# Four 3x3 convolutions: from direct taps over whole images to row-pair combinations over strips of 16 rows

## The chip, the cores and the metric

The kernel runs on one core of a Trainium2 chip. Time is device microseconds of that core, from three runs of the kernel before and one profiled execution. A core has a matrix engine (TensorE, PE in the profile; its weight loads are PEld), a vector engine (VectorE, DVE), a scalar engine (ScalarE, ACT), a general engine (GpSimd, POOL), and a queue engine (SyncE, SP), which here issues all transfers. TensorE reads SBUF and writes PSUM, which has eight banks of 512 float32 words on each of 128 partitions.

## The reference

The input `x` is 4 images of 64 channels and 128x128 pixels in float32. Four layers follow each other, and only the third and the head of the fourth are touched:

```
layer 0   a state-space layer over the pixels        x  -> x1
layer 1   windowed transforms and small matrices     x1 -> x2
layer 2   r = relu(bn(conv3x3(x2)));  r = relu(bn(conv3x3(r)))
          sums over the squares r[j:, j:], j = 0..64; their means, a 3-wide
          filter over channels, a sigmoid, a mean over j:  gate per image and channel
          x3 = relu(r * gate + x2)
layer 3   y = relu(conv3x3(x3));  t = conv3x3(y)      (64 -> 64 channels, padding 1)
          a state-space layer over t, then a feed-forward layer, then + x3
```

So four 3x3 convolutions of 64 to 64 channels are computed on four images. The gate needs the whole result of the second before the third can begin.

## The kernel before

The layers run one after another, with memory (DRAM) between them. `layer2_convs3` holds layer 2 and the two convolutions of layer 3. Images go in pairs: 2 images x 64 channels lie on the 128 partitions. Two buffers of a whole padded image pair (130 x 130 words on each partition) stand in SBUF, and the convolutions go from one to the other and back (`a` and `bb`).

`_conv` (line 1184) takes 8 rows at a time. For each of the nine taps it issues four matmuls of 64x64 weights by 512 pixels: two images (the two row halves of the array) by two groups of four rows (the two column halves). Nine taps add up in PSUM. The function `done` takes the result out: for the first three convolutions ACT writes relu(scale * p + bias) into the other image buffer (line 1258), for the fourth DVE adds the bias (line 1316), and 16 rows at a time are stored.

Between the second and the third convolution of a pair stands the gate. DVE takes the sums over the square rings, one row part (line 1283) and one column part (line 1284) for each of 64 rings, and one block (line 1280). A cumulative sum, a matmul with a band matrix and a sigmoid give a number for each partition. Then 8 rows at a time are fetched from memory again (line 1303), multiplied and added (line 1304), rectified in place (line 1305) and stored as `x3` (line 1306). The third convolution starts as soon as its first rows are there.

The program is recorded as a flow of tiles. A planner then sets the order of instructions on each engine, by data, by the buffers that are free and by its own estimate of when something is ready. An engine runs its instructions in that order and waits at each until its data are there. All transfers are issued by SP in one order, so a transfer that waits holds back those behind it.

Of the kernel before, what the change touches and what calls it, by code (L numbers as in the profile page):

```python
# [10 lines left out]
F32 = mybir.dt.float32  # L11
AF = mybir.ActivationFunctionType
ALU = mybir.AluOpType
AX = mybir.AxisListType
PSUM = bass.MemoryType.PSUM
DRAM = bass.MemoryType.DRAM

P = 128
B, C, HH, WW = 4, 64, 128, 128
# [97 lines left out]
class _Consts:  # L117


    def __init__(self, nc, pool, cst, upto=None):  # L120
        w = _OFF[upto][1] if upto else _CONST.shape[1]
        self.t = pool.tile([P, w], F32, name="cst")
        nc.sync.dma_start(self.t, cst[:, :w])
# [14 lines left out]
def _rstd(nc, out, in_, eps):  # L138

    nc.scalar.activation(out, in_, AF.Ln, bias=eps)  # L140
    nc.scalar.activation(out, out, AF.Exp, scale=-0.5)
# [29 lines left out]
class _Mamba:  # L171
# [119 lines left out]
    def rows(self, bc, h, k):  # L291

        a = 64 * h + DD * k if self.small else 64 * (h ^ k)
        return bc[a : a + self.nst, :512] if self.small else bc[a : a + self.nst, _COLS[h]]
# [365 lines left out]
    def gated(self, c):  # L660

        yg = self.tmp("yg")
        self.nc.vector.tensor_mul(yg, c["y"], c["sz"])
        return yg
# [514 lines left out]


RW = WW + 2


def _conv(tc, pool, W, src, done):

    nc = tc.nc
    half = [slice(64 * h, 64 * (h + 1)) for h in range(2)]
    for r in range(0, HH, 8):  # L1190
        p = [pool.tile([P, 4, WW], F32, name=f"cv{i}", tag=f"cv{i}") for i in range(2)]
        for k in range(9):
            dy, dx = divmod(k, 3)
            for h in range(2):
                at = r + 4 * h + dy
                for i in range(2):
                    nc.tensor.matmul(  # L1197
                        p[i][half[h]],
                        W[half[i], k, :],
                        src[half[i], at : at + 4, dx : dx + WW],  # L1200
                        start=k == 0,
                        stop=k == 8,
                    )
        for i in range(2):
            for h in range(2):
                done(i, r + 4 * h, h, p[i][half[h]])


@with_exitstack
def layer2_convs3(ctx, tc, K, w, w3, x2, x3, t3):  # L1210
    nc = tc.nc
    cp = ctx.enter_context(tc.tile_pool(name="l2c", bufs=1))
    wp = ctx.enter_context(tc.tile_pool(name="l2w", bufs=3))
    cv = ctx.enter_context(tc.tile_pool(name="l2p", bufs=3, space=PSUM))
    sm = ctx.enter_context(tc.tile_pool(name="l2s", bufs=1, space=PSUM))

    wts = []
    for src in (w["c1"], w["c2"], w3["c1"], w3["c2"]):
        t = cp.tile([P, 9, C], F32, name=f"cw{len(wts)}")
        for h in range(2):  # L1220
            nc.sync.dma_start(t[64 * h : 64 * (h + 1)], src)
        wts.append(t)
    eps = cp.tile([P, 1], F32, name="eps2")
    nc.vector.memset(eps, 1e-5)
    norms = []
    for i in "12":
        g, b, m, v, cb = (
            _dup(nc, cp, w[k], f"{k}_") for k in (f"bn{i}_g", f"bn{i}_b", f"bn{i}_m", f"bn{i}_v", f"c{i}_b")
        )
        _rstd(nc, v, v, eps)  # L1230
        nc.vector.tensor_mul(g, g, v)
        nc.vector.tensor_sub(cb, cb, m)
        nc.vector.tensor_mul(cb, cb, g)
        nc.vector.tensor_add(cb, cb, b)
        norms.append((g, cb))
    bias3 = [_dup(nc, cp, w3[k], f"{k}3") for k in ("c1_b", "c2_b")]
    eca = cp.tile([P, 3], F32, name="eca")
    nc.sync.dma_start(eca, w["eca"].to_broadcast([P, 3]))
    band = cp.tile([P, P], F32, name="band")
    nc.vector.tensor_scalar(band, K.sh0, eca[:, 0:1], None, ALU.mult)  # L1240
    nc.vector.scalar_tensor_tensor(band, K.sh1, eca[:, 1:2], band, ALU.mult, ALU.add)
    nc.vector.scalar_tensor_tensor(band, K.sh2, eca[:, 2:3], band, ALU.mult, ALU.add)

    bufs = []
    for i in range(2):
        t = cp.tile([P, HH + 2, RW], F32, name=f"img{i}")
        nc.gpsimd.memset(t[:, 0:1, :], 0.0)
        nc.gpsimd.memset(t[:, HH + 1 : HH + 2, :], 0.0)
        nc.gpsimd.memset(t[:, :, 0:1], 0.0)
        nc.gpsimd.memset(t[:, :, RW - 1 : RW], 0.0)  # L1250
        bufs.append(t)
    a, bb = bufs
    ain, bin_ = (t[:, 1 : HH + 1, 1 : WW + 1] for t in bufs)

    def into(dst, func, scale, bias):
        def done(i, r, h, p):
            at = slice(64 * h, 64 * (h + 1))
            nc.scalar.activation(
                dst[64 * i : 64 * (i + 1), r : r + 4, :],
                p,  # L1260
                func,
                scale=scale if isinstance(scale, float) else scale[at],
                bias=bias[at],
            )

        return done

    NSUM = HH // 2 + 1
    for pr in range(B // 2):
        img2 = x2[2 * pr : 2 * pr + 2].rearrange("b c (r w) -> (b c) r w", w=WW)  # L1270
        img3 = x3[2 * pr : 2 * pr + 2].rearrange("b c (r w) -> (b c) r w", w=WW)
        for r in range(0, HH, 32):
            nc.sync.dma_start(ain[:, r : r + 32, :], img2[:, r : r + 32, :])
        _conv(tc, cv, wts[0], a, into(bin_, AF.Relu, *norms[0]))
        _conv(tc, cv, wts[1], bb, into(ain, AF.Relu, *norms[1]))


        part = wp.tile([P, 2, NSUM], F32, name="part", tag="part")
        nc.vector.memset(part[:, 1, 0:1], 0.0)
        nc.vector.tensor_reduce(part[:, 0, 0:1], ain[:, HH // 2 :, WW // 2 :], AX.XY, ALU.add)  # L1280
        for i in range(1, NSUM):
            j = HH // 2 - i
            nc.vector.tensor_reduce(part[:, 0, i : i + 1], ain[:, j, j:], AX.X, ALU.add)
            nc.vector.tensor_reduce(part[:, 1, i : i + 1], ain[:, j + 1 :, j], AX.X, ALU.add)
        add = wp.tile([P, NSUM], F32, name="add", tag="add")
        nc.vector.tensor_add(add, part[:, 0, :], part[:, 1, :])
        sq = wp.tile([P, NSUM], F32, name="sq", tag="sq")
        nc.vector.tensor_tensor_scan(sq, K.ones[:, :NSUM], add, 0.0, ALU.mult, ALU.add)

        nc.vector.tensor_mul(sq, sq, K.iarea)  # L1290
        py = sm.tile([P, NSUM], F32, name="py", tag="py")
        nc.tensor.matmul(py, band, sq, start=True, stop=True)
        sg = wp.tile([P, NSUM], F32, name="sg", tag="sg")
        nc.scalar.activation(sg, py, AF.Sigmoid)
        nc.vector.tensor_mul(sg, sg, sq)
        gate = wp.tile([P, 1], F32, name="gate", tag="gate")
        nc.vector.tensor_reduce(gate, sg, AX.X, ALU.add)
        nc.vector.tensor_scalar_mul(gate, gate, 1.0 / NSUM)

        for r in range(0, HH, 8):  # L1300
            rows = slice(r, r + 8)
            res = wp.tile([P, 8, WW], F32, name="res2", tag="res2")
            nc.sync.dma_start(res, img2[:, rows, :])
            nc.vector.scalar_tensor_tensor(res, ain[:, rows, :], gate, res, ALU.mult, ALU.add)
            nc.scalar.activation(ain[:, rows, :], res, AF.Relu)
            nc.sync.dma_start(img3[:, rows, :], ain[:, rows, :])

        _conv(tc, cv, wts[2], a, into(bin_, AF.Relu, 1.0, bias3[0]))
        tok = t3[2 * pr : 2 * pr + 2].rearrange("b c (r w) -> (b c) r w", w=WW)
        stage = {}  # L1310

        def store(i, r, h, p):
            at = slice(64 * h, 64 * (h + 1))
            if r % 16 == 0 and i == 0:
                stage["t"] = wp.tile([P, 16, WW], F32, name="tok", tag="tok", bufs=2)
            nc.vector.tensor_scalar(
                stage["t"][64 * i : 64 * (i + 1), r % 16 : r % 16 + 4, :], p, bias3[1][at], None, ALU.add
            )
            if r % 16 == 12 and i == 1:
                nc.sync.dma_start(tok[:, r - 12 : r + 4, :], stage["t"])  # L1320

        _conv(tc, cv, wts[3], bb, store)

# [105 lines left out]
def layer3_ffn(ctx, tc, K, w, n3, s3, out):  # L1431
# [46 lines left out]
    def first(b, r0, H):  # L1478
# [15 lines left out]
        for t in (1, 0):  # L1494
            himg = H[t] = wp.tile([P, R + 2, RW], F32, name=f"h{t}", tag=f"h{t}")
            nc.gpsimd.memset(himg[:, :, 0:1], 0.0)  # L1496
            nc.gpsimd.memset(himg[:, :, RW - 1 : RW], 0.0)
            if r0 == 0:
# [210 lines left out]
```

## Time and profile before

| | us |
|---|---|
| median of 3 runs | 17,647.88 (17,646.33 to 17,652.58) |
| profiled execution, its time | 17,656.56 |
| its span, first to last instruction | 17,654.7 |
| convolution stage, first to last matmul of line 1197 | 4332.8 to 5418.7 |
| PE busy in the span | 14,230.1 |
| DVE busy | 15,333.9 |
| ACT busy | 14,311.2 |
| POOL busy | 13,820.2 |

How to read a row of the groups of instructions: line of the kernel, engine, operation, tile written <- tiles read (partitions x elements), count; then busy time in us and the mean of one in ns; then the time that its engine sat idle just before, and what ended most of that. Up to about 3,160 us the span belongs to layer 0, from 5,422 us on to the rest of layer 3, both with DVE, ACT and POOL busy most of the time.

### The profile page before, as it was taken

The numbers are of one execution on the slowest core, as the hardware profiler recorded it, in microseconds if no ns is written. First come the engines' busy times: TensorE is split into PE (matmuls) and PEld (weight loads), VectorE is DVE, ScalarE is ACT, GpSimd is POOL, SyncE is SP. The second block draws the span as 40 slices with busy tenths as digits, with TensorE's granted clock in tenths as the row PEclk, the third lists the DMA queues.
The fourth block names the chain that finished last, engine by engine and source line by source line (L and its number), as shares of the span: only waits on it lengthen the run. The fifth ranks groups of instructions, "written<-read, shape, count | busy, mean of one in ns | idle before, by whom it ended". The sixth has DMA issues, their size and how long they took to land. (4 is left out here: it accounts for less than half of the span.)

```text
span 17654.7 us, 242673 instructions
## 1 busy us (share of the span) xinstructions
PE 14230.1 (81%) x82490; PEld 6984.1 (40%) x82490; DVE 15333.9 (87%) x8623; ACT 14311.2 (81%) x29985; POOL 13820.2 (78%) x7966
## 2 busy tenths in 40 slices
PE   7888888798997777777777777777777777777799
PEld 3333333387334333333333333333333333333333
DVE  8999999522216999999999999999999999999977
ACT  8999999112335999999999999999999999999733
POOL 7999999200005999999999999999999999999700
PEclk8888888799998999999999999999999999999899
DMA  6766666111212333333333333333333333333222
GB/s 160 179 179 178 175 179 177 51 61 45 72 41 79 89 90 91 88 93 85 93 85 94 83 95 84 94 86 91 87 91 86 93 87 91 89 90 91 69 59 55
DMA packets 669699, 1723.23 MB, mean 98 GB/s; under 512 B 196816, under 2 KB 232096, under 8 KB 661024
## 3 DMA queue, kind: packets, MB, share of 16 engines
q1 hardware_dynamic: 668448, 1707.69, 36.0%
q8 instruction: 646, 10.58, 0.3%
q14 instruction: 605, 4.96, 0.1%
HBM read 1434.33 MB, written 272.63 MB: 97 GB/s over the span
## 5 line engine op out<-in xcount | busy, mean ns | idle before, releaser
L632 POOL TENSOR_TENSOR ring<-ring,cb 128x1024 f32<-128x1024 f32 x5120 | 12038.9, 2381 | 335.4 <-DVE ring L626 186.1
L626 DVE TENSOR_TENSOR_SCAN ring<-da,state,bx 128x1024 f32<-128x1024 f32 x4848 | 11053.0, 2327 | 70.8 <-PE y L457 38.1
L431 ACT ACTIVATE bxT<-duT,BT 128x128 f32<-128x128 f32 x21504 | 6706.0, 389 | 29.9 <-PE bx L514 28.1
L582 ACT ACTIVATE da<-dl,A 128x1024 f32<-128x1024 f32 x5120 | 5751.0, 1139 | 168.1 <-DVE ring L626 115.2
L514 PE MATMUL bx<-cst,bxT 128*128 128x128 f32 x24576 | 3693.7, 300 | 945.1 <-DVE ring L626 641.6
L514 PEld LDWEIGHTS bx<-cst,bxT 128*128 128x128 f32 x24576 | 3248.7, 209 | 2341.9 <-DVE ring L626 1523.1
L520 PE MATMUL bx<-bc,spread 64*128 64x512 f32 (+1 forms) x8192 | 2401.2, 684 | 1439.2 <-DVE ring L626 1427.9
L457 PE MATMUL y<-ring,cst 128*32 128x512 f32 x20480 | 3030.3, 675 | 120.8 <-POOL ring L632 120.1
L526 DVE TENSOR_TENSOR bx<-du,bx 128x1024 f32<-128x1024 f32 x2048 | 2463.1, 1211 | 301.3 <-PE bx L520 183.8
L520 PEld LDWEIGHTS bx<-bc,spread 64*128 64x128 f32 (+1 forms) x8192 | 690.2, 195 | 2819.0 <-DVE ring L626 2305.6
L457 PEld LDWEIGHTS y<-ring,cst 128*32 128x32 f32 x20480 | 633.3, 119 | 2040.0 <-issue 1433.7
L1197 PE MATMUL cv<-img,cw 64*64 64x512 f32 x9216 | 1009.3, 595 | 73.2 <-DMA img<-d_x 45.5
L300 PE MATMUL bx<-S,cw 128*128 128x512 f32 x1024 | 663.2, 806 | 367.9 <-DVE ring L626 354.5
L1355 POOL MEMSET X<- 64x1 f32 x4 | 0.4, 97 | 1122.2 <-DMA cw<-in_l_conv_wT 1122.2
L435 POOL TENSOR_TENSOR bxT<-duT,BT 128x512 f32<-128x512 f32 x768 | 808.3, 1053 | 10.1 <-ACT BT L381 10.1
L1122 POOL TENSOR_TENSOR xs<-xs,cl 128x1024 f32<-128x1024 f32 x32 | 76.0, 2374 | 860.8 <-DVE cl L1121 860.8
L1496 POOL MEMSET h<- 128x18 f32 x64 | 8.3, 132 | 875.2 <-PE pd L1584 443.5
L1197 PEld LDWEIGHTS cv<-img,cw 64*64 64x64 f32 x9216 | 435.1, 134 | 645.5 <-issue 537.8
L1510 ACT ACTIVATE h<-ph,ff_fc_b 128x384 f32<-128x384 f32 (+1 forms) x384 | 201.1, 578 | 593.2 <-PE ph L1505 593.2
L1584 PE MATMUL pd<-h,diag 64*64 64x512 f32 x4608 | 632.0, 603 | 0.7 <-issue 0.7
L626 DVE TENSOR_TENSOR_SCAN ring<-da,bx 128x1024 f32<-128x1024 f32 x272 | 604.8, 2268 | 9.4 <-PE y L457 5.8
L1530 DVE SCALAR_TENSOR_TENSOR g<-h,dww,g 128x2048 f32<-128x2048 f32 x256 | 601.9, 2351 | 11.0
(314 smaller groups left out, 9963.3 us busy)
## 6 DMA issues: line engine op xcount, KB each, us to landing
cb<-c SPq DMA_DIRECT2D x5120, 128.0 KB, 2.8
dl<-d SPq DMA_DIRECT2D x2048, 128.0 KB, 3.3
du<-d SPq DMA_DIRECT2D x2048, 128.0 KB, 3.7
d<-pos SPq DMA_DIRECT2D x128, 512.0 KB, 3.7
d<-u SPq DMA_DIRECT2D x128, 512.0 KB, 3.9
X<-d_t SPq DMA_DIRECT2D x124, 256.0 KB, 4.1
S<-in_x SPq DMA_DIRECT2D x120, 256.5 KB, 4.5
res<-in_x SPq DMA_DIRECT2D x128, 128.0 KB, 3.0
```

The lines of the kernel that those rows point to most:

```text
L300: self.nc.tensor.matmul(out[: l.shape[1], k : k + 512], l, r[:, k : k + 512], start=i == 0, stop=i == len(pairs) - 1)
L431: nc.scalar.activation(t[:, k, q].rearrange("p e j -> p (e j)"), c["duT"][:, k, :], AF.Copy, scale=c["BT"][:, k, n : n + 1])
L435: nc.gpsimd.tensor_mul(t[:, k].rearrange("p q e j -> p q (e j)"), c["duT"][:, k].unsqueeze(1).to_broadcast(shape), c["BT"][:, k, NQ * g : ...
L457: nc.tensor.matmul(c["y"][DD * j : DD * (j + 1), _COLS[h]], K.sel, hc[:, _COLS[h]], start=False, stop=u["g"] == self.ng - 1,)
L514: nc.tensor.transpose(bx[:, P * m : P * (m + 1)], v["bxT"][:, m, :, :, j].rearrange("p q e -> p (q e)"), self.K.eye)
L520: nc.tensor.matmul(bx[:, _COLS[h]], self.spread[v["g"]][r], self.rows(v["c"]["B"], h, 0), start=True, stop=True)
L526: nc.vector.tensor_mul(tiles[k], v["c"]["du"][j], tiles[k])
L582: nc.scalar.activation(das[nexp], v["c"]["dl"][k], AF.Exp, scale=self.A[:, k, v["g"] : v["g"] + 1])
L626: nc.vector.tensor_tensor_scan(hs, das.pop(i), tiles[i], 0.0 if u["c"].get("reset") else st, ALU.mult, ALU.add)
L632: nc.gpsimd.tensor_mul(hc, hs, u["cb"])
L1197: nc.tensor.matmul(p[i][half[h]], W[half[i], k, :], src[half[i], at : at + 4, dx : dx + WW], start=k == 0, stop=k == 8,)
L1584: nc.tensor.matmul(pd[i][half[h]], diag[half[i], k, :], h0[half[i], r : r + 4, dx : dx + WW], start=k == 0, stop=k == 8,)
```

## The change

A pair of output rows of a 3x3 convolution is computed from four input rows r0..r3. For each of the three taps along a row, direct computing needs six products for the pair (three taps of height, two rows). The new code forms four combinations of rows, V0 = r0 - r2, V1 = r1 + r2, V2 = r2 - r1, V3 = r1 - r3, and four of the weights (made once at the start, in `weights`), takes four products m0..m3, and puts together y0 = m0 + (m1 + m2), y1 = m3 + (m1 - m2); the sign of m3 is in its weights. Three taps along the row add up in PSUM as before.

Work goes in strips of 16 rows instead of whole images. `turned` makes V of a strip: V1 and V0 on DVE, V2 and V3 on POOL. `product` issues 48 matmuls into eight PSUM tiles of one buffer each. `back` copies m1 on ACT and makes sums, differences and y on DVE. A strip carries a row more above and below: the first convolution loads them from memory, between two convolutions POOL copies them from strip to strip (`between`). The second convolution follows two strips behind the first, the fourth two behind the third. The second's result goes to memory (`rd`) and DVE takes its ring sums strip by strip (`summed`). A second pass over both pairs loads `rd` and `x2` again, multiplies by the gate, rectifies and stores `x3` (`source`), and then runs the third and fourth convolution. V of the next unit is recorded ahead of `back` of the present one, loads three strips ahead.

```diff
-def _conv(tc, pool, W, src, done):
-    for r in range(0, HH, 8):
-        p = [pool.tile([P, 4, WW], F32, name=f"cv{i}", tag=f"cv{i}") for i in range(2)]
-        for k in range(9):
-            dy, dx = divmod(k, 3)
-            for h in range(2):
-                at = r + 4 * h + dy
-                for i in range(2):
-                    nc.tensor.matmul(p[i][half[h]], W[half[i], k, :],
-                        src[half[i], at : at + 4, dx : dx + WW], start=k == 0, stop=k == 8)
...
+SR = 16
+NP = SR // 4
+class _Conv:
+    KS = (1, 2, 0, 3)
+    def __init__(self, ctx, tc):
+        self.vp = ctx.enter_context(tc.tile_pool(name="cvv", bufs=2))
+        self.ep = ctx.enter_context(tc.tile_pool(name="cve", bufs=2))
+        self.pp = ctx.enter_context(tc.tile_pool(name="cvp", bufs=1, space=PSUM))
+    def weights(self, cp, src, name):
+        t = self.vp.tile([P, 3, 3, C], F32, name="cwraw", tag="cwraw")
...
+        u = cp.tile([P, 4, 3, C], F32, name=name)
+        nc.vector.tensor_copy(u[:, 0], t[:, 0])
+        nc.vector.tensor_scalar_mul(u[:, 3], t[:, 2], -1.0)
+        nc.vector.tensor_add(t[:, 0], t[:, 0], t[:, 2])
+        nc.vector.tensor_add(u[:, 1], t[:, 0], t[:, 1])
+        nc.vector.tensor_sub(u[:, 2], t[:, 0], t[:, 1])
+        nc.vector.tensor_scalar_mul(u[:, 1:3], u[:, 1:3], 0.5)
+    def turned(self, X):
+        V = self.vp.tile([P, 4, SR // 2, RW], F32, name="V", tag="V")
+        r = [X[:, k : k + SR - 1 : 2, :] for k in range(4)]
+        nc.vector.tensor_add(V[:, 1], r[1], r[2])
+        nc.gpsimd.tensor_sub(V[:, 2], r[2], r[1])
+        nc.vector.tensor_sub(V[:, 0], r[0], r[2])
+        nc.gpsimd.tensor_sub(V[:, 3], r[1], r[3])
+    def product(self, V, U):
+        for k in self.KS:
+            p[k] = [self.pp.tile([P, NP, WW], F32, name=f"m{k}{i}", tag=f"m{k}{i}") for i in range(2)]
+            for x in range(3):
+                for h in range(2):
+                    for i in range(2):
+                        self.nc.tensor.matmul(p[k][i][half[h]], U[half[i], k, x, :],
+                            V[half[i], k, NP * h : NP * (h + 1), x : x + WW], start=x == 0, stop=x == 2)
+    def back(self, p, bias=None):
+        y = self.ep.tile([P, 2, NP, 2, WW], F32, name="y", tag="y")
+        sd = self.ep.tile([P, 2, 2, NP, WW], F32, name="sd", tag="sd", bufs=1)
+        for i in range(2):
+            one = self.ep.tile([P, NP, WW], F32, name="one", tag="one")
+            nc.scalar.copy(one, p[1][i])
+            nc.vector.tensor_add(sd[:, i, 0], p[2][i], one)
+            nc.vector.tensor_sub(sd[:, i, 1], one, p[2][i])
+        for k in range(2):
+            for i in range(2):
+                if bias is None:
+                    nc.vector.tensor_add(y[:, i, :, k], p[3 * k][i], sd[:, i, k])
+                else:
+                    nc.vector.scalar_tensor_tensor(y[:, i, :, k], p[3 * k][i], bias, sd[:, i, k], ALU.add, ALU.add)
...
+    def load(kind, pr, s):
+        X = strip("X", s, 3)
+        if kind == 0:
+            nc.sync.dma_start(X[:, at, 1 : WW + 1], img2[pr][:, of, :])
+            return X
+        r, x = (wp.tile([P, SR + 2, WW], F32, name=n, tag="r", bufs=4) for n in ("rin", "xin"))
+        nc.sync.dma_start(r[:, at, :], rd[pr][:, of, :])
+        nc.sync.dma_start(x[:, at, :], img2[pr][:, of, :])
+        return X, r, x
+    def source(kind, pr, s, got):
...
+        nc.vector.scalar_tensor_tensor(r[:, at, :], r[:, at, :], gates[pr], x[:, at, :], ALU.mult, ALU.add)
+        nc.scalar.activation(X[:, at, 1 : WW + 1], r[:, at, :], AF.Relu)
+        nc.sync.dma_start(img3[pr][:, SR * s : SR * (s + 1), :], X[:, 1 : SR + 1, 1 : WW + 1])
+    def spread(y, dst, scale, bias):
+        for i in range(2):
+            for h in range(2):
+                nc.scalar.activation(dst[half[i], SR // 2 * h : SR // 2 * (h + 1), :],
+                    y[half[h], i].rearrange("p n k w -> p (n k) w"), AF.Relu, ...)
+    def between(kind, pr, s, y):
+        t = mid((pr, kind), s)
+        spread(y, t[:, 1 : SR + 1, 1 : WW + 1], scale, bias)
+        if s:
+            nc.gpsimd.tensor_copy(mid((pr, kind), s - 1)[:, SR + 1, 1 : WW + 1], t[:, 1, 1 : WW + 1])
+        if s < NS - 1:
+            nc.gpsimd.tensor_copy(mid((pr, kind), s + 1)[:, 0, 1 : WW + 1], t[:, SR, 1 : WW + 1])
+    def summed(pr, s, y):
+        r = wp.tile([P, SR + 2, WW], F32, name="r", tag="r", bufs=4)[:, :SR]
+        spread(y, r, *norms[1])
+        nc.sync.dma_start(rd[pr][:, SR * s : SR * (s + 1), :], r)
...
+        if top:
+            nc.vector.tensor_reduce(cols[:, s, NSUM - top :],
+                r[:, :, :top].rearrange("p r c -> p c r")[:, ::-1, :], AX.X, ALU.add)
+        if top == HH // 2:
+            nc.vector.tensor_reduce(cols[:, s, 0:1], r[:, :, top:], AX.XY, ALU.add)
+            return
+        for k in range(SR):
+            nc.vector.tensor_reduce(line[:, 0, at], r[:, k, j:], AX.X, ALU.add)
+            if k < SR - 1:
+                nc.vector.tensor_reduce(cols[:, s, at], r[:, k + 1 :, j], AX.X, ALU.add)
...
+    def out(pr, s, y):
+        for i in range(2):
+            for h in range(2):
+                nc.sync.dma_start(tok[pr][half[i], r0 : r0 + SR // 2, :], y[half[h], i].rearrange("p n k w -> p (n k) w"))
+    units = []
+    for first in (0, 2):
+        for pr in range(B // 2):
+            for s in range(NS + 2):
+                units += [(first, pr, s)] if s < NS else []
+                units += [(first + 1, pr, s - 2)] if s > 1 else []
+    fetch(2)
+    V = {0: cv.turned(source(*units[0], got[units[0]]))}
+    for n, (kind, pr, s) in enumerate(units):
+        p = cv.product(V.pop(n), wts[kind])
+        fetch(loads.index((kind, pr, s)) + 3 if kind in (0, 2) else 0)
...
+        if n + 1 < len(units):
+            u = units[n + 1]
+            if u[0] == 2 and u[1] not in gates:
+                gated(u[1])
+            V[n + 1] = cv.turned(source(*u, got.get(u)))
+        y = cv.back(p, bias3[1] if kind == 3 else None)
...
```

The other layers are not touched.

## The prediction

> **What bounds the kernel now.** I read the convolution stage in stretches of time, then the groups of instructions with each shape apart, then two places in order of time. In the stretches the columns are length, then busy time and record count of PE, PEld, DVE, ACT and POOL, then granted TensorE clock, DMA share and GB/s.
>
> ```profile
> 4332.80:4450.00 117.20, 117.20 (x1068) 46.61 (x1072) 0.00 (x0) 43.43 (x56) 0.00 (x0) 0.98 0.18 52
> ...
> 4583.00:4611.00 28.00, 0.76 (x8) 0.53 (x6) 23.49 (x74) 5.67 (x7) 0.00 (x0) 0.58 0.00 0
> 4611.00:4660.00 49.00, 40.40 (x322) 14.24 (x326) 16.38 (x13) 20.10 (x22) 0.00 (x0) 0.86 0.90 280
> 4660.00:4850.00 190.00, 187.82 (x1744) 66.56 (x1740) 37.28 (x49) 39.40 (x57) 0.00 (x0) 1.00 0.28 90
> ...
> 4332.80:5418.70 1085.90, 1010.69 (x9220) 436.12 (x9220) 198.69 (x426) 321.51 (x419) 0.00 (x0) 0.96 0.18 59
> ```
>
> The last row is the whole stage, 1085.9 us of the 17,654.7 us span: PE is busy for 1010.7 us of it, DVE for 199, POOL for none. TensorE bounds this stage and nothing else comes near. The second row is the gate of the first image pair, with TensorE idle; the third, just behind it, is the only one held by memory: 280 GB/s at a share of 0.90. In the fourth, undisturbed, 1744 records take 187.82 us. A float32 matmul leaves two records (9216 for the 4608 of line 1197), so one costs 2 x 107.7 = 215.4 ns[...].
>
> The prices of what the change adds come from these groups:
>
> ```profile
> L1153 DVE TENSOR_TENSOR X<-X,p 128x1024 f32<-128x1024 f32 x32 | 39.1, 1221 | 245.2 <-PE p L1146 245.2
> ...
> L950 DVE SCALAR_TENSOR_TENSOR Z<-pk,eye 128x256 f32<-128x256 f32 x27 | 11.4, 423 | 35.2 <-PE pk L948 35.2
> ...
> L1316 DVE TENSOR_SCALAR tok<-cv,c_b 64x512 f32<-64x512 f32 x128 | 96.0, 750 | 338.1 <-PE cv L1197 336.2
> ...
> L1530 DVE SCALAR_TENSOR_TENSOR g<-h,dww,g 128x2048 f32<-128x2048 f32 x256 | 601.9, 2351 | 11.0
> ...
> L1258 ACT ACTIVATE img<-cv,c_b__29111,bn_g__29099 64x512 f32<-64x512 f32 x128 | 99.3, 776 | 147.9 <-PE cv L1197 146.1
> ...
> L1402 ACT COPY tx<-bx 128x512 f32<-128x512 f32 x64 | 37.5, 586 | 271.2 <-PE bx L672 271.2
> ...
> L344 POOL TENSOR_TENSOR u<-pos,xc 128x1024 f32<-128x1024 f32 x128 | 303.5, 2371 | 63.7 <-ACT pos L336 63.7
> ```
>
> Between 256 elements (423) and 1024 (1221) DVE's cost grows 1.04 ns an element, so 512 cost 0.69 us; a scalar read from a tile adds 0.06 (750 at line 1316).
>
> **The change, part by part.** A unit is one strip of 16 rows of one image pair in one convolution: 4 x 2 x 8 = 64 units.
>
> *TensorE.* Four row combinations by three taps by four quarters: 48 matmuls a unit where 72 stood. 3072 x 0.2154 = 662 us instead of 992: 330 us go, from the path that sets the end. The idle at the two gates (28 us each) goes with it, since the sums are now taken strip by strip; the turnovers below stand in its place.
>
> *DVE.* Per unit two V combinations of 1040 elements (1.23 each, 2.5) and eight instructions on 128x512 (0.69 each, 5.5): 8.0 us. Each of 16 third-convolution units adds one multiply-add of 2304 elements, 2351 + 256 x 1.04 = 2.6 us. A second-convolution strip in the upper half adds 16 row sums (246 ns by line 1283), 15 short column sums (line 1284 falls 2 ns an element from 326 at 95, so about 0.16 us) and a block sum: 7.1 us. In the lower half it is 3.1. In all 64 x 8.0 + 16 x 2.6 + 8 x 7.1 + 8 x 3.1 + 4 = 640 us, against 199. That is almost TensorE's 662.
>
> *ACT.* Two copies (0.59 each), four spreads of 64x1024 (776 + 430 more for 512 more elements, from 685 and 1115 ns at lines 1258 and 1375: 1.2 each): 6.0 a unit, some 335 us. *POOL.* Two V combinations, 2.4 each: 310 us. Both hide behind TensorE's 10.3 us a unit by their sums; what matters is the ring. PSUM has eight banks and the unit uses all, with one buffer each: the next unit's second group of matmuls (k = 2) waits for DVE's four sum-and-difference instructions, these wait for ACT's copies, which stand on ACT behind the spreads of the unit before, and these wait for DVE's last y.
>
> In ordinary units the ring closes in time: from DVE's last y, two spreads (2.4) and a copy (0.6) pass while DVE makes V (2.5), then 5.5: about 9 us. Behind an upper-half second-convolution strip it doesn't. For the two units DVE has 2 x 8.0 + 7.1 = 23.1 us, plus about 2 us in which it waits for the copies, against 20.7 on TensorE: some 4.2 us lost, eight times, 34 us. At the end of each pass three second-convolution units follow each other, with about 6 us lost twice. Together **46 us**.
>
> *Turnovers.* Before the first third-convolution unit of a pair TensorE stands idle. First pair: band matmul 0.7, sigmoid with its table 1.5, the spreads of two strips that waited for buffers 8 x 1.2, rectifier 2.1, V on DVE and POOL 3.6: 17.5 us. Second pair: no spreads queue there and the multiply-add is on the chain: 0.7 + 0.5 + 0.6 + 2.6 + 2.1 + 3.6 = 10. With what the restarts at a low clock cost (below), 4 us each, **36 us**.
>
> *Loads.* The second pass fetches r and x again and stores the gated strip: 2 x 18 and 16 rows of 64 KB, 2.36 + 1.05 MB a strip, on SP's queue. In the built order of instructions all of it is crowded to the start of a pair: on DVE the multiply-add of strip 7 stands ahead of the sums of the fourth unit (first pair) and of the last y of the third (second pair). For it, five full strips and a shorter one must have landed, 14.0 MB, with six stores between them, 6.3 MB: 20.3 MB at 281 GB/s (third row above, the same mix of loads and 512-byte stores) is 72 us, and its last load must still be used. TensorE can do four units in that time, 41 us; then its banks are not freed. Some 35 us lost per pair, **73 us**. Were memory to give 250 or 320 GB/s, 20 more or 14 fewer. The y stores that stand behind on SP come late but have only y's two buffers behind them.
>
> *The port of DVE and POOL.* Here the trace shows what V will meet:
>
> ```profile
> 3301.91 3.60 POOL L811 TENSOR_TENSOR m<-h 128x2048 f32<-128x2048 f32 x1 [2.31 <-DVE h L808]
> ...
> 3303.86 3.76 DVE L808 TENSOR_TENSOR h<-X 128x2016 f32<-128x2016 f32 x1
> ```
>
> DVE's addition of two SBUF tiles starts under POOL's and ends 2.1 us after it, though alone it takes 2.26. It stood still for POOL's instruction. From the row alone every DVE instruction of the change might be so delayed, 640 us of work. The Trainium skill, "SBUF — State Buffer", section "Who interferes with whom", narrows it: only a DVE instruction with both inputs in SBUF locks against a POOL instruction that reads SBUF. Then sums, differences and y, with one input in PSUM, are free, and V and the multiply-add pay. No run here tests that limit. By it V takes up to 2 x 1.23 + 2 x 2.4 = 7.3 us and not 2.5, but two thirds lie in the time in which DVE would wait for the copies: I add 9 us, included in the 46. Bounds: 0, and 160 (below, second rival).
>
> *The clock.* Behind the gate's gap TensorE ran for 4 us at half speed (weight loads 0.85 us apart until 4615, then 0.43); the stretch with short gaps after it was granted 0.86. By that row, all 662 us would become 770. The skill, "TensorE: Matmul & The Clock Gate", Part 1, says that the clock falls to half after about 3.4 us without work and comes back after about as long: only gaps beyond that count. I see about ten, at the turnovers and in the loads, so 10 x 1.7 = 17 us, of which most lies under waits; I take 4 us for each turnover, 2 for the start. Bounds 0 and 50, as half of the 108 would be hidden.
>
> *Start and end.* Weights are turned (24 short DVE instructions, under 8 us) while the last store of the layer before lands; before, the first image load was issued at 4322.8 and matmuls began at 4332.8; 17 rows in place of 32 land some 5 us sooner, two weight loads now stand ahead of that store (2.5 us), and V takes 2.4 back: 5 us earlier. At the end the last two y (1.5 us) stand where four bias additions (3.0) stood, and four stores where one stood: nothing. All other layers keep their order of instructions.
>
> **Sum.** 662 + 46 + 36 + 73 + 2 = 819, and 8 for hand-offs too short to list: 827 us where 1086 were, with the start 264 saved. The profiled execution took 17,656.6 us, 1.9 more than its span: 17,392. It lies 0.05% above the median of the runs, 17,647.9, so the forecast is **17,385 us**, 1.5% faster.
>
> **The rivals.**
> - *Loads don't hold anything* (8%). If DVE and memory keep pace in the second pass, 73 goes: 746 us, 17,303. For it: a share of 0.28 in most of the stage; against it: 0.90 at the gate with half of these bytes.
> - *VectorE becomes the bound* (10%). If V costs 7.3 us in every unit, with nothing of it under waits, DVE holds 640 + 64 x 4.8 = 947 us, and with the turnovers 983: 103 + 5 saved, 17,541. For it: 3044 ns in the middle for line 808 against 2258 at least; against: DVE mostly finds POOL half done.
> - *Slower* (2%). The half clock stays: the ring's waits, one in nearly every unit, keep TensorE from ever being counted as busy. At half clock 2 x 662 plus the turnovers is 1360: 17,917. It decides from a mean clock of about 0.62 downwards. Against it: layers with gaps everywhere were granted 0.91 to 0.93.
>
> **How the numbers follow.** 80% for the forecast; its range adds the bounds: DMA -14 to +20, clock to +50, port to +30, sums -10 (block sums at 1.1 ns an element), and what I missed: 17,330 to 17,465. The three rivals are the 20% left out. A measurement of this kernel tells about 0.2% (35 us) from no change: faster 0.97, same 0.01, slower 0.02.
>
> **What would show it.** Stage near 827 us from its first to its last matmul; 6144 matmul records; DVE near 700 us busy in it with V's mean well above 1.23; TensorE waiting for DVE's sums behind each upper-half strip; DMA at 0.9 for some 75 us twice, with DVE's multiply-add waiting for it. Wrong if the units behind the turnovers run at 10.3 us, or ordinary units take over 11.

## The result and the profile after

| | before | after |
|---|---|---|
| median of 4 runs (of before, the three above and one more) | 17,648.81 us (17,646.33 to 17,652.58) | 17,330.46 us (17,327.46 to 17,333.99) |
| profiled execution | 17,656.6 us | 17,333.1 us |
| stage, first to last matmul of the convolutions | 1085.9 us | 774.0 us |

The ratio is 0.9818, with a 95% interval of 0.9803 to 0.9834. The change saves 318 us where 264 were forecast: the direction is right, and the time lies on the low edge of the range (17,330). Nearly all of the 54 us between them is in the stage, 774 us where 827 were forecast. The two profiled executions lie 323.5 us apart: 312 in the stage, 7 in its start, which came at 4325.7 us instead of 4332.8, and 4.5 behind it. Such small parts can't be read as effects: in the profiles of the kernels below the untouched layers behind the stage took from 6 us less to 5 us more than here, and the stage began between 4324.0 and 4329.9. So single kernels are compared below by the length of the stage.

First the stage of the changed kernel in stretches. The columns are those of the same table of before: length, busy time and records of PE, PEld, DVE, ACT and POOL, granted clock, DMA share, GB/s.

```profile
4706.60:4771.00 64.40, 54.27 (x385) 25.19 (x385) 55.63 (x47) 32.80 (x29) 31.73 (x25) 0.89 0.98 351
...
4786.50:4905.90 119.40, 110.89 (x1034) 52.37 (x1026) 109.14 (x114) 38.78 (x45) 56.30 (x54) 0.98 0.28 85
4905.90:4986.00 80.10, 65.86 (x480) 29.10 (x484) 60.69 (x56) 29.69 (x28) 31.67 (x28) 0.92 0.79 276
...
4325.70:5099.70 774.00, 714.00 (x6148) 355.54 (x6148) 660.31 (x938) 335.20 (x339) 347.82 (x311) 0.96 0.41 135
```

TensorE is busy for 714 of 774 us, DVE for 660. The second row is a plain stretch of third and fourth convolutions (with 9 us of the next turnover at its end). The first and third are the stretches behind the two turnovers: few matmuls for their length, and a DMA share of 0.98 in one, 0.79 in the other.

Then the groups of the stage, each shape apart:

```profile
L1232 PE MATMUL m<-V,cw 64*64 64x512 f32 x6144 | 713.3, 603 | 101.2 <-POOL V L1218 67.4 <-DVE sd L1250 16.9 <-ACT one L1248 13.3
...
L1254 DVE TENSOR_TENSOR y<-m,sd 128x512 f32<-128x512 f32 x192 | 120.5, 682 | 5.2 <-PE m L1232 4.1
L1220 POOL TENSOR_TENSOR V<-X 128x1040 f32<-128x1040 f32 x32 | 96.3, 3010 | 0.0
L1249 DVE TENSOR_TENSOR sd<-m,one 128x512 f32<-128x512 f32 x128 | 87.5, 684 | 61.4 <-ACT one L1248 49.1 <-PE m L1232 12.1 <-issue 0.3
...
L1348 ACT ACTIVATE mid<-y,c_b__29123,bn_g__29111 64x1024 f32<-64x1024 f32 x64 | 79.4, 1240 | 102.1 <-DVE y L1254 101.1
...
L1219 DVE TENSOR_TENSOR V<-X 128x1040 f32<-128x1040 f32 x32 | 76.7, 2396 | 0.0
...
L1248 ACT COPY one<-m 128x512 f32<-128x512 f32 x128 | 68.6, 588 | 119.5 <-PE m L1232 118.5
...
L1217 DVE TENSOR_TENSOR V<-X 128x1040 f32<-128x1040 f32 x32 | 57.4, 1792 | 3.2 <-DMA X<-d_x 2.9 <-issue 0.3
...
L1340 DVE SCALAR_TENSOR_TENSOR rin<-rin,gate,xin 128x2304 f32<-128x2304 f32 x12 | 35.1, 2926 | 19.0 <-DMA xin<-d_x 19.0
```

The 6144 matmul records are those of 3072 matmuls. The prices hold: 0.68 us for DVE's 512 elements (0.69 forecast), 1.24 for a spread (1.2), 0.59 for a copy. V is prolonged: 1.8 and 2.4 us in these two rows, where undisturbed ones took 1.23. The multiply-add waited 19 us for its load. TensorE's waits, of the same stage:

```profile
PE m L1232 <- POOL V L1218: 67.4, 3, 41.2
PE m L1232 <- DVE sd L1250: 16.9, 25, 3.8
PE m L1232 <- ACT one L1248: 13.3, 6, 3.9
```

41.2 of the 67.4 lie before the stage's first matmul, the others are the two turnovers. From the starts of the 64 units (the first matmul of each) the balance can be made. A plain unit takes 10.3 us: 64 x 10.3 = 659. What units take beyond that: 28 for those around second-convolution strips (0.6 to 2.3 each, and one of 8.0 at the end of the first pair); 32 at the turnovers (18.7 and 9.5 in the unit before, nearly all of it idle, and 2.4 and 1.8 in the unit after); 49 in the four units behind each turnover (12 to 22 us each); 3.4 in the first unit. Together 772 of 774.

### The profile page after: what moved, and what is told of

It is laid out like the page before. It is cut to its first block, busy times and chain, and to the rows that moved or that the text cites. A ratio compares the mean times of both kernels' runs of the same rounds, so it can differ in the third digit from the quotient of the medians.

```text
span 17331.3 us, 238151 instructions
## 1 busy us (share of the span) xinstructions
PE 13927.6 (80%) x79418; PEld 6901.8 (40%) x79418; DVE 15802.2 (91%) x9155; ACT 14324.0 (83%) x29905; POOL 14169.2 (82%) x8290
## 5 line engine op out<-in xcount | busy, mean ns | idle before, releaser
L1232 PE MATMUL m<-V,cw 64*64 64x512 f32 x6144 | 713.3, 603 | 101.2 <-POOL V L1218 67.4
L300 PEld LDWEIGHTS bx<-S,cw 128*128 128x128 f32 x1024 | 256.0, 263 | 787.5 <-DVE ring L626 464.8
L1232 PEld LDWEIGHTS m<-V,cw 64*64 64x64 f32 x6144 | 355.0, 136 | 457.6 <-issue 273.9
```

What stands on the lines that cost most here:

```text
L300: self.nc.tensor.matmul(out[: l.shape[1], k : k + 512], l, r[:, k : k + 512], start=i == 0, stop=i == len(pairs) - 1)
L1232: self.nc.tensor.matmul(p[k][i][half[h]], U[half[i], k, x, :], V[half[i], k, NP * h : NP * (h + 1), x : x + WW], start=x == 0, stop=x == 2,)
```

## Experiments

The theory under test: what is left beside TensorE's 659 us is not work but order. The multiply-adds of later strips stand on DVE ahead of sums that free PSUM banks, and the ring sums stand ahead of them likewise. The main rivals: memory itself holds the second pass; DVE's work, with V prolonged by POOL, fills the units. Where a kernel adds lines, its line numbers move: the changed kernel's line 1340 is line 1348 of the first.

### One edge of order for the multiply-add

```diff
+    def after(key):
+        ins = nc.cur_bb.bb.instructions[-1]
+        if key in ends:
+            why = mybir.DependencyInfo(mybir.DependencyClass.NoSync, mybir.DependencyReason.DATA)
+            tc.add_manual_dep(ins, ends[key], why, reason="order")
...
         nc.vector.scalar_tensor_tensor(r[:, at, :], r[:, at, :], gates[pr], x[:, at, :], ALU.mult, ALU.add)
+        after(units.index((kind, pr, s)) - 1 - 2)
...
         y = cv.back(p, bias3[1] if kind == 3 else None)
+        ends[n] = nc.cur_bb.bb.instructions[-1].name
```

> One edge of order added and nothing else: DVE's multiply-add of a gated strip (line 1340 of the changed kernel) may not stand ahead of the last y of the unit three before the one that uses it. Same bytes, same instructions. Theory: the units behind the two turnovers (12 to 22 us each where 10.3 is the plain unit, 49 us lost in the eight of them) are slow because multiply-adds of strips needed much later stand on DVE ahead of the sums that free the PSUM banks. Then about 45 us come back: stage 729 us where the changed kernel took 774, time about 17,286. Rival: memory has to deliver the same strips at the same time anyway and the wait only moves to V: stage 765 to 774, time 17,321 to 17,331.

Measured: 17,290.07 us median of 4 (17,283.56 to 17,296.27), ratio to before 0.9797 (0.9781 to 0.9813); the stage took 729.5 us. 44.5 us came back, by an edit that removes no byte and no instruction:

```profile
4325.50:5055.00 729.50, 692.62 (x6148) 388.53 (x6148) 645.16 (x939) 336.07 (x339) 329.96 (x311) 0.97 0.44 143
```

The four units behind the first turnover take 13.1, 11.3, 10.3 and 10.3 us (13.1, 16.9, 21.7 and 12.1 before the edit), those behind the second 10.3 each (18.0, 19.0, 19.0, 12.0). How it comes about is seen on DVE in order of time (start, length, line, and in brackets the idle time before and its releaser). The changed kernel, with the sums of the second and the third unit of the second pass:

```profile
4730.32 3.43 DVE L1219 TENSOR_TENSOR V<-X 128x1040 f32<-128x1040 f32 x1
4733.68 2.64 DVE L1340 SCALAR_TENSOR_TENSOR rin<-rin,gate,xin 128x2304 f32<-128x2304 f32 x1
4736.24 0.68 DVE L1249 TENSOR_TENSOR sd<-m,one 128x512 f32<-128x512 f32 x1
...
4745.31 1.23 DVE L1219 TENSOR_TENSOR V<-mid 128x1040 f32<-128x1040 f32 x1
4750.63 4.35 DVE L1340 SCALAR_TENSOR_TENSOR rin<-rin,gate,xin 128x2304 f32<-128x2304 f32 x1 [4.09 <-DMA xin<-d_x]
4754.91 0.68 DVE L1249 TENSOR_TENSOR sd<-m,one 128x512 f32<-128x512 f32 x1
```

The same place with the edge:

```profile
4730.20 3.44 DVE L1219 TENSOR_TENSOR V<-X 128x1040 f32<-128x1040 f32 x1
4733.56 0.68 DVE L1249 TENSOR_TENSOR sd<-m,one 128x512 f32<-128x512 f32 x1
...
4739.50 1.23 DVE L1219 TENSOR_TENSOR V<-mid 128x1040 f32<-128x1040 f32 x1
4740.65 2.61 DVE L1348 SCALAR_TENSOR_TENSOR rin<-rin,gate,xin 128x2304 f32<-128x2304 f32 x1
4743.23 0.69 DVE L1249 TENSOR_TENSOR sd<-m,one 128x512 f32<-128x512 f32 x1
```

Without the edge, DVE stood for 4.09 us before one multiply-add and then took 4.35 for it, while the sums of the third unit, which free the banks for TensorE's next group, stood behind it; their products were there, for they start at once when it is done, at 4754.91. With the edge the sums of the same unit (the last row) start at 4743.23, and no multiply-add of that kernel waits for a load at all.

### A small second load

```diff
-        nc.sync.dma_start(x[:, at, :], img2[pr][:, of, :])
+        nc.sync.dma_start(x[:, :2, :], img2[pr][:, of, :][:, :2, :])
...
-... gates[pr], x[:, at, :], ALU.mult, ALU.add)
+... gates[pr], x[:, :1, :].to_broadcast([P, at.stop - at.start, WW]), ALU.mult, ALU.add)
```

> Left out: 15 or 16 of the 17 or 18 rows of x2 in each load of the second pass; the multiply-add takes one row for all (the output is then not the layer's). All buffers and instructions stay. The crowded stretch carries some 13 MB where it carried 20.3. By bytes over rate (13 MB at the 351 GB/s seen there is 37 us, less than the 41 us that TensorE takes for four units) the loss goes: stage about 727 us. Theory of order: the multiply-adds run as far ahead as their buffers allow, whatever the bytes, and DVE stands still for a strip's buffers as it stood for its load: stage 762 to 774.

Measured: one run of 17,326.79 us, stage 768.6. Fewer bytes brought 5 us. But the edit is not clean: the planner put the multiply-adds still further ahead, probably because it expected the loads sooner, and they waited 17.4 us for loads, against 22.5. So bytes and order were parted by holding the order.

### The small load with the old order, and with the edge

The first of these two kernels holds each multiply-add behind the DVE instruction that it followed in the changed kernel:

```diff
+        place = {
+            (0, 2): (32, "sd"), (0, 3): (34, "V"), (0, 4): (33, "sd"), (0, 5): (35, "V"), (0, 6): (34, "sd"), (0, 7): (36, "V"),
+            (1, 2): (49, "V"), (1, 3): (48, "y0"), (1, 4): (50, "V"), (1, 5): (49, "y0"), (1, 6): (51, "V"), (1, 7): (50, "y0"),
+        }
+        if (pr, s) in place:
...
+            tc.add_manual_dep(ins, ends[place[pr, s]], why, reason="order")
```

The second has the edge of the first experiment in its place.

> As the small second load (one or two rows of x2 in place of 17 or 18, one of them used for all rows), and twelve edges of order hold each multiply-add behind the DVE instruction that it followed in the changed kernel, so that it no longer moves further ahead. This parts the 49 us of the eight units behind the turnovers into bytes and order. If DVE only waited for bytes, 13 MB at 351 GB/s take 37 us against TensorE's 41 and nothing is lost: stage 727. If only for buffers: 774. Theory: both, since a strip's buffers come free only when earlier strips have been rectified and turned: stage 755, 19 us of bytes and 30 of order.

> As the small second load, with the edge of order of the first experiment (multiply-add behind the y of three units before). Theory: with the multiply-adds in their place no unit waits for a load, and the bytes are worth nothing: stage 727 to 730, as the 729.5 of the edge with all bytes. Rival, that bytes are a cost of their own: stage 705 to 715.

Measured: one run each, 17,316.33 us with a stage of 759.5, and 17,285.99 with 728.6. The rows of the first (its stage, and the stretch behind its first turnover), then the stage of the second:

```profile
4325.80:5085.30 759.50, 706.91 (x6148) 358.26 (x6148) 660.38 (x938) 335.25 (x339) 347.48 (x311) 0.96 0.37 116
4706.80:4764.00 57.20, 50.46 (x384) 22.97 (x384) 53.78 (x46) 31.64 (x27) 30.70 (x25) 0.93 0.89 287
...
4329.90:5058.50 728.60, 691.21 (x6148) 379.81 (x6148) 644.02 (x938) 336.17 (x339) 327.83 (x311) 0.97 0.38 121
```

With the order held, the bytes are worth 14.5 of the 49 us, and another 30 go only with the order. (The stretch carried 57.2 us x 287 GB/s = 16.4 MB, more than the 13 reckoned in the expectation; at 351 GB/s that is 47 us, still 10 less than the stretch took.) With the multiply-adds in their place the bytes are worth 1 us (728.6 against 729.5), so the rival of a cost of their own falls.

Over half of these 30 us shows in DVE's instructions of the first of these kernels (its line 1345 is the multiply-add, 1251 the first of the sums):

```profile
4738.80 2.61 DVE L1345 SCALAR_TENSOR_TENSOR rin<-rin,gate,xin 128x2304 f32<-128x2304 f32 x1
...
4746.02 2.61 DVE L1345 SCALAR_TENSOR_TENSOR rin<-rin,gate,xin 128x2304 f32<-128x2304 f32 x1
4748.80 0.69 DVE L1251 TENSOR_TENSOR sd<-m,one 128x512 f32<-128x512 f32 x1 [0.17 <-ACT one L1250]
...
4753.24 2.75 DVE L1345 SCALAR_TENSOR_TENSOR rin<-rin,gate,xin 128x2304 f32<-128x2304 f32 x1 [1.96 <-DMA xin<-d_x]
...
4760.61 2.48 DVE L1345 SCALAR_TENSOR_TENSOR rin<-rin,gate,xin 128x2176 f32<-128x2176 f32 x1
```

Its multiply-adds hardly wait any more. Idle time of DVE before them in the stage, in us, and how often, in the changed kernel and then here:

```profile
DMA xin<-d_x: 22.5, 10
...
DMA xin<-d_x: 3.7, 5
```

Still 34.5 of the 49 us are lost. The multiply-adds are too many in one place. Into the four units behind each turnover the order puts six and five of them, 31.4 us of DVE; with the edge three and two stand there, 13.0 us. DVE is busy 16.5 us longer in these eight units than with the edge. The other 13 are idle time of DVE, 7.6 of it waits for ACT's copies, while TensorE was granted a clock of 0.94 and 0.88 in these units (1.00 with the edge); how much a slower TensorE adds to the loss is not parted here.

What holds the transfers where memory is not full shows in the queue of SP in the second stretch of the changed kernel, 4905.9 to 4986.0 us:

```profile
SPq L1342 <- ACT X L1341: 35.3, 5, 17.6
SPq L1328 <- DVE V L1219: 10.4, 3, 8.9
```

Line 1342 is the store of a gated strip. It stands on SP ahead of loads of later strips, waits for the rectifier, and the loads wait with it. That this wait by itself costs TensorE time was not tried apart; with DVE waiting only 3.7 us for loads in the kernel above, late loads can't be most of the 30.

### Without ring sums, and with some of them twice

```diff
-        if top:
+        if top and s < 0:
...
         if top == HH // 2:
-            nc.vector.tensor_reduce(cols[:, s, 0:1], r[:, :, top:], AX.XY, ALU.add)
             return
-        for k in range(SR):
+        for k in range(0):
```

> Left out: all ring sums of the second convolution's strips (both loops of reduces, lines 1381 to 1393); the gate is computed from zeros. Theory: they cost what the second-convolution units are longer than 10.3 us, about 10 and 8 us in the two pairs, and some 8 us at the end of the first pair: stage 746 to 750 us. Rival: V, prolonged by POOL, is what holds these units: stage above 764. By the forecast's own price (4.2 us for each of eight upper strips and 6 twice) 728.

The other kernel has `for k in [*range(SR), *range(SR)]` in this last line and changes nothing else.

> The 16 row sums and 15 column sums of each upper-half strip are taken twice (same values, written again): 31 DVE instructions more in eight strips. DVE has no slack there, so their cost is all seen. By the mean durations of the forecast (16 x 246 ns and 15 x 0.16 us: 6.3 us a strip) the stage grows by 51 to 825 us. If instructions that follow each other start 0.08 us before the record of the one before ends, by 6.3 - 31 x 0.08 = 3.8 us a strip: by 31 to 805. Rival, that the sums lie in DVE's free time: under 10, below 784.

Measured, one run each: 17,303.62 us with the sums left out, 17,364.05 with the small ones twice. The two stages:

```profile
4328.60:5070.00 741.40, 691.04 (x6148) 331.69 (x6148) 662.63 (x659) 335.25 (x339) 369.56 (x311) 0.96 0.42 140
```

```profile
4329.60:5136.50 806.90, 725.62 (x6148) 376.91 (x6148) 700.24 (x1186) 335.24 (x339) 351.19 (x311) 0.94 0.39 129
```

Without them every unit of the first pass takes 10.3 us, save the first and the one before the turnover, and the stage is 32.6 us shorter: 30 us in the first pass, as the balance says. V was there in both, so V alone does not hold these units; whether it adds to what the sums cost is not parted here. With 248 more reduces the stage grew by 32.9 us: 4.1 us a strip, near the 3.8 of the reading that a DVE instruction costs less than its record lasts, and not the 6.3 of the mean durations. Part of this nearness is luck: the units of the eight upper strips grew by 39 us, others became 6 shorter, and V's records on DVE were 13 us longer in sum. The changed kernel's own trace shows the cost directly, at the sums of one upper strip:

```profile
4439.04 2.48 DVE L1254 TENSOR_TENSOR y<-m,sd 128x512 f32<-128x512 f32 x4
...
4448.48 0.22 DVE L1391 TENSOR_REDUCE sum<-r 128x1 f32<-128x70 f32 x1
4448.61 0.15 DVE L1393 TENSOR_REDUCE sum<-r 128x1 f32<-128x5 f32 x1
4448.68 0.22 DVE L1391 TENSOR_REDUCE sum<-r 128x1 f32<-128x69 f32 x1
4448.81 0.15 DVE L1393 TENSOR_REDUCE sum<-r 128x1 f32<-128x4 f32 x1
...
4449.58 0.68 DVE L1249 TENSOR_TENSOR sd<-m,one 128x512 f32<-128x512 f32 x1
4450.18 0.68 DVE L1250 TENSOR_TENSOR sd<-one,m 128x512 f32<-128x512 f32 x1
```

The records last 0.22 and 0.15 us but start 0.13 and 0.07 us after each other. Four y of 0.68 take 2.48 together, not 2.73. A DVE instruction that waits for nothing starts about 0.08 us before the record of the one before it ends. From start to start a strip's 31 small reduces hold DVE for 3.4 to 4.1 us, where their records sum to 5.8 to 6.5.

### All of V on DVE

```diff
-        nc.gpsimd.tensor_sub(V[:, 2], r[2], r[1])
+        nc.vector.tensor_sub(V[:, 2], r[2], r[1])
...
-        nc.gpsimd.tensor_sub(V[:, 3], r[1], r[3])
+        nc.vector.tensor_sub(V[:, 3], r[1], r[3])
```

> V2 and V3 made on DVE as well, nothing on POOL for them. In the changed kernel DVE spent 57.4 + 76.7 us on the 64 instructions of V1 and V0, 2.10 us each where the shortest took 1.23: POOL's instruction on the same port holds it. Theory: freed of that, four instructions of about 1.2 us cost DVE 4.8 us a unit where two cost 4.2, so DVE has little more to do: V's mean falls to under 1.3 us and the stage is 770 to 790 us. Rival, that POOL takes work off DVE as its share says: 2.5 us more in every unit, and in the 32 units of the first two convolutions, where DVE has no slack, 2 x 16 x 2.5 = 80 us: stage over 830.

Measured: one run of 17,340.57 us, stage 780.5. The groups of one of V's lines on DVE there, and of one that was POOL's:

```profile
L1219 DVE TENSOR_TENSOR V<-X 128x1040 f32<-128x1040 f32 x32 | 39.8, 1242 | 0.0
L1218 DVE TENSOR_TENSOR V<-X 128x1040 f32<-128x1040 f32 x32 | 39.7, 1242 | 0.0
```

With POOL out of the way line 1219 takes 1.24 us and not 2.4. The eight groups of V together hold DVE for 318 us; in the changed kernel the four of DVE held it for 248. So POOL's 319 us of work took 70 off DVE, and 6.5 off the stage. That is as expected if DVE and POOL hold each other up; the rival's 80 us did not come.

### Two taps instead of three

```diff
-            for x in range(3):
+            for x in range(2):
...
-                            stop=x == 2,
+                            stop=x == 1,
```

> Left out: the third tap along the row in every product, 16 of a unit's 48 matmuls (the output is then not the convolution). TensorE needs 64 x 6.9 = 440 us. Theory: DVE stands close behind it: with 640 to 660 us of its own work in the stage and the ring through ACT the stage ends at 670 to 710 us, and plain units take 8 to 9 us. Rival, that only TensorE and the listed stalls set the pace: 774 - 219 = 555 us, plain units 6.9.

Measured: one run of 17,253.08 us, stage 699.5 us. A third less work for TensorE brings 74 us of 219: plain units take 7.4 and 9.6 in turn in the second pass, about 10.0 in the first. TensorE's longest sums of waits in that stage:

```profile
PE m L1232 <- ACT one L1248: 76.3, 44, 4.2
PE m L1232 <- POOL V L1218: 68.2, 3, 41.1
```

So what stands close behind TensorE is the ring, not DVE by its sum alone: ACT's copies, queued behind the spreads of the unit before. In the full kernel a plain unit of 10.3 us still covers it, in the first pass by 0.3 us.

### The edge with early gates, and then with later sums

The first of the two kernels lets the multiply-add stand one unit earlier than the edge did (four units ahead in place of three) and records each gate away from the turnover; the second also puts the sums of a strip one unit later, and the first gate two strips later, since it needs them.

```diff
+        after(units.index((kind, pr, s)) - 1 - 3)
...
-            if u[0] == 2 and u[1] not in gates:
-                gated(u[1])
...
+        if (kind, pr, s) in ((0, 1, 1), (2, 0, 2)):
+            gated(kind // 2)
```

```diff
+        owed.append((units.index((1, pr, s)) + 1, lambda: reduced(pr, s, r)))
...
-        if (kind, pr, s) in ((0, 1, 1), (2, 0, 2)):
+        if (kind, pr, s) in ((0, 1, 3), (2, 0, 2)):
...
+        while owed and owed[0][0] <= n:
+            k = len(nc.cur_bb.bb.instructions)
+            owed.pop(0)[1]()
+            first = next(i for i in nc.cur_bb.bb.instructions[k:] if i.engine == mybir.EngineType.DVE)
+            why = mybir.DependencyInfo(mybir.DependencyClass.NoSync, mybir.DependencyReason.DATA)
+            tc.add_manual_dep(first, ends[n], why, reason="order")
```

(`reduced` is the part of `summed` that takes the sums.)

> The edge of order of the first experiment, one unit further ahead (four units), and the gate of each pair recorded early: that of the first pair behind unit (0, 1, 1), that of the second behind (2, 0, 2), so that neither stands at a turnover. Theory: of the 28 us in which TensorE is idle at the two turnovers the second's 9.4 and its 2 us of restart go, of the first's 18.6 some 10; 22 us less than with the edge alone: stage 707, time 17,264. Rival, that the strips' own chain (multiply-add, rectifier, V: 8.3 us behind the last unit) sets the turnover whatever the gate: under 8 us less, stage above 721.

> As the kernel before it in this list, and the ring sums of a strip recorded one unit later, with an edge of order that puts them behind the last y of that next unit. Same instructions. DVE's work in the stage (some 660 us) is less than the stage's length, so the sums can lie in the time in which DVE waits for the products of the next unit but one. Theory: most of the 28 us that the sums cost go: stage 686, time 17,242. Rival, that DVE has no free time in the two-unit cycle of an upper strip (2 x 8 + 4.6 us in 20.6) and its end moves out as before: stage 700 to 707.

Measured: 17,261.57 us (17,259.14 to 17,267.66), ratio to before 0.9781 (0.9764 to 0.9797), and 17,250.47 us (17,248.21 to 17,253.89), ratio 0.9775 (0.9761 to 0.979); four runs each. Their stages:

```profile
4328.60:5036.80 708.20, 691.89 (x6148) 309.66 (x6148) 640.59 (x938) 336.30 (x339) 354.57 (x311) 0.98 0.45 147
```

```profile
4329.10:5015.50 686.40, 679.53 (x6148) 304.18 (x6148) 636.07 (x938) 336.27 (x339) 354.53 (x311) 0.99 0.47 152
```

Both stages came out as the theory said (707 and 686 us). The second kernel's median is 8 us above the expected 17,242; the layers behind the stage took 5 us more in its profile than in that of the changed kernel, the size of the drift named above. The second turnover is gone in both: all units around it take 10.3 us. The edge of the sums acts only on the first reduce of a strip, the block of columns; the 31 small ones stayed where they were. Most of the gain is at the ends of the pairs, where the sums of three strips follow each other: the unit that took 19.1 us at the end of the first takes 10.3. This kernel is 80 us faster by its median than the changed one, by the place of instructions alone; gate, multiply-add and sums were not moved one by one.

## Why the prediction was right and wrong

What the change saves on TensorE was right, and so were the places of the losses. The sizes of two losses failed, and one of these in its mechanism too. Against the forecast stage of 827 us the measured one is shorter by 24 in the loads, 18 in DVE's sums, 4 at the turnovers and 3 on TensorE; of 8 for hand-offs 2 were found, and the first unit cost 1 more. All large errors point the same way, and the range allowed 31 for what it had not listed; without that it would have ended 31 above the measured time.

**TensorE**, 662 us: right, 64 x 10.3 = 659. **Start**, 5 us: 7, but the start moved by 6 between kernels that share its code. **Turnovers**, 36 us: 32; the idle times forecast as 17.5 and 10 were 18.7 and 9.5, and the restarts cost 2.4 and 1.8, not 4 each. With the gate early and the multiply-add a unit sooner the second turnover vanished, as the chain says; the two were not tried apart.

**Loads**, 73 us: 49. The place held, multiply-adds ahead of sums, and one edge of order gave back 44.5. The failed step is to reckon this loss as bytes over a rate: "20.3 MB at 281 GB/s (third row above, the same mix of loads and 512-byte stores) is 72 us, and its last load must still be used." The rate was too low. Memory gave 351 GB/s at a share of 0.98, and up to 436 in single slices of 2.5 us; the bound of 320 was passed (and by the forecast's own sum 320 makes 18 us less, not 14). It was not the same mix either: a packet carried 843 bytes in the mean in the row of before, 1,592 behind the first turnover, where less was stored. The Trainium skill had the better bound: "Perfetto Trace Analysis", section "Roofline", says that 358 GB/s is a core's share and that a core working alone can get up to about 435, the limit of its 16 DMA engines. This trace agrees with it. At 351 the 20.3 MB take 58 us, 28 less for both pairs, about the miss of 24.

But that agreement is luck, for the second pair ran at 276 GB/s, as slowly as forecast, and lost 27 us, not 36. The mechanism was wrong in its larger part. With the same order and 28% fewer bytes only 14.5 of the 49 us went, though DVE then waited 3.7 us for loads and not 22.5. The rest is the order itself: DVE does six and five multiply-adds in the four units behind a turnover, with their load there or not. The forecast let DVE stand at one multiply-add until the bytes were there and gave the time of the others no term.

**DVE and the ring**, 46 us: 28 by the balance, 32.6 by leaving the sums out. The upper strips lost 13 us where 34 were forecast; the ends of the pairs lost 15, where 12 were. The failed step is the price of the sums, "246 ns by line 1283 ... about 0.16 us ... 7.1 us". The durations were right, 240 and 152 ns in the median, but an instruction's record is not its cost: the 31 small reduces start 0.08 us early each, 2.5 us a strip. The row of before that gave the 246 is a mean of records; only instructions in order of time show the distance between starts. The Trainium skill states it: "Vector Engine (DVE) Microarchitecture Reference", section 5.2, gives 1.0417 ns a column and about 75 ns an instruction after queue overlap, measured there on 32-bit integers, which for 512 columns is 608 ns, an estimate that the 0.60 us between starts confirms; the 0.68 us of the records is not it. Less 2.5, the forecast's 4.2 us for an upper strip become 1.7, within the 0.6 to 2.3 measured. That is not a full account: the sums, differences and y also follow each other at 0.60 and not 0.69, and V takes longer than the 1.23 forecast in this sum.

**The port of DVE and POOL**, 9 us: the trace confirms who is hit. V's records went up to 3.46 us, while sums, differences and y, with one input in PSUM, stayed between 667 and 701 ns in all 448 instructions without a scalar, as the rule named in the prediction limits it. Its own share of the stage could not be measured apart; all of V on DVE, without POOL beside it but with more work, is 6.5 us slower.

**What would show it.** TensorE's waits for DVE's sums came behind each upper strip, plain units took 10.3 us, V was well above 1.23. DVE's busy time was 660 us, not near 700. DMA at 0.9 for 75 us came as 64 us at 0.98 and 80 at 0.79. Of the rivals VectorE as the bound did not come, nor the half clock: 0.96 was granted in the stage. That the loads hold nothing (17,303; 827 less 73 is 754, so by its own sum 17,312) was nearer to the measured time than the forecast, but wrong in cause: the units behind the turnovers lost 49 us. What remains open is the part of the order that is not DVE's own work, some 13 of 30 us, and what SP's waiting stores cost.

## What to carry to other kernels

When a planner lets work of later tiles run ahead on an engine that also frees the buffers of the present one, look at the order before the bytes: here one edge of order gave 44.5 us, and fewer bytes 5, or 14.5 with the order held. Such work costs its own time there, even when its data have come. Price a row of short DVE instructions by the distance of their starts in order of time, not by the mean of their records; and take a rate from a stretch as a limit only where the share was full and the transfers were of the same kind.

## What the runs showed of the hardware that was not expected

A DVE record that nothing holds overlaps the one before by about 0.08 us: reduces of 0.22 and 0.15 us pass in pairs of 0.20. On ACT four spreads of 1.24 us took 5.02 and overlap in nothing, while two copies of 0.59 from PSUM took 1.07.

POOL as a helper for two-input work from SBUF gave DVE little: 319 us of POOL's time spared 70 of DVE's.
